# Two transformer layers on one core: reordering the first permutes and norms, gated up products together, first queries on GpSimd, sigmoid by tanh

## Chip, cores and metric

The kernel runs on one core of one Trainium2 chip. The metric is the device time of one execution in microseconds (us); lower is better. An engine is named as the profile names it: PE (TensorE, matmuls), PEld (its weight loads), DVE (VectorE), ACT (ScalarE), POOL (GpSimd), SP (SyncE, which only issues DMAs here).

## The reference, cut to what matters

Two layers act on x of 2 batches x 1024 tokens x 256 features, all in float32. Each layer adds an attention and a feed-forward branch of the same normalized x:

```python
xn = _layernorm(x)
x = x + _L0_attn_ref(xn, ...) + _L0_ffn_ref(xn, ...)
xn = _layernorm(x)
x = x + _L1_attn_ref(xn, ...) + _L1_ffn_ref(xn, ...)
```

Layer 0's attention has 16 heads of width 16 with a causal mask. The reference reshapes the projected (tokens, features) matrix straight into (heads, tokens, 16), so that a head is a block of 64 tokens with all features; the kernel has to permute. Layer 0's feed-forward uses ternary weights (the sign times the mean magnitude of a group of 64), a squared relu and an rms norm. Layer 1's attention is latent: queries from 192 and keys and values from 64 latent columns, 16 heads, rotary positions on 64 columns of each head. Layer 1's feed-forward quantizes its three weights to -1, 0 and 1 and computes

```python
hidden = jax.nn.sigmoid(x @ w1q.T) * (x @ w2q.T)
return hidden @ w3q.T
```

## The kernel before

Tokens lie in 16 tiles of 128 rows (0 to 7 are batch 0, 8 to 15 are batch 1), kept in `x_sb`. The program is one hand-written order: each call issues its instructions at that place into the in-order queues of the engines, and Tile adds the semaphores. An engine that waits therefore holds back everything that was issued to it later. PSUM is handed out as three single banks (`ps_bank`, tile `ps_m`), two pairs (`ps_pair`, `ps_s`) and one accumulator (`ps_o`).

**The start.** Statistics of x (`ln_stat`: two DVE instructions a tile), their square root on ACT (`ln_root`), the reciprocal on DVE (`ln_rstd`), the normalized tile (`ln_norm`, two tiles at once, into the single buffer `xn`; on POOL for most of the head), and its transposes on PE with the copy to `xnT` on ACT (`ln_turn`). `project(g, i)` computes keys (i=1), queries (0) or values (2) of head group g and writes them to DRAM (`rows`); `fetch` reads them back in head order into `stage`; `permute` copies them to `head` tiles. Group g reads only even tiles of its batch for the first two groups and only odd ones for the next two. `first_w` and `second_w` are the four steps (`begin`, `scale`, `choose`, `put`) that make a piece of layer 0's feed-forward weights ternary.

**The first maxima.** Layer 0's softmax takes two passes: `maxima` (PE scores, then DVE reductions to `nmx`), later `scores` with the exponential on ACT, and `product` with the values. A loop over groups g runs from -1 and in it over n = 0 to 11; it computes the maxima of group g+1 beside the scores of group g. At g = -1 there are only maxima, and the dictionary `first` lists for each n what is issued with them: turns and norms of the remaining tiles, projections, `fetch` and `permute`, and eight ups of layer 0's feed-forward. An up is PE products, three ACT passes (relu, square, square) and an accumulation on POOL (`acc`, L541). The four steps of two more weight pieces are dealt over n as well, after the entry of `first`.

**The fill.** From g = 0 on, a list `fill` supplies one piece of independent PE work a step: projections, layer 0's feed-forward, and from g = 5 layer 1's feed-forward of batch 0 (`ffn1(0)`, `ffn1(1)`, 512 tokens each). `ffn1(n)` has 12 ups (six columns, each as product with w1, sigmoid on ACT, product with w2, multiplication on DVE) and 8 downs (six products each, added to `x_sb` on DVE).

**Between the layers.** After the last product of layer 0 a loop over eight tiles of batch 1 does `project_out`, takes pieces of `fill`, and takes pieces of `side`: `down1` (the latent products of layer 1, one tile each). Then batch 1 is normalized and turned, `ffn1(2)` and `ffn1(3)` become the fill, and `side` holds the rest of layer 1's preparation: `norms1` and `keys1` (mostly POOL), `queries1` (transposes), `fold` (products of weights, each with DMA loads two folds ahead), `turn_keys`. When few pieces of fill are left, the buffer of w1 is given to the encoding weights `wpe` and the tables of cosines, and the first two queries are issued: `project` (32 matmuls), copies on ACT, and `rotate` (two multiplications and four additions of pieces, on the engines that it is given).

**Layer 1's attention** loops over 16 steps of pairs of token blocks: scores, maxima on DVE, exponential on ACT, 32x32 transposes on DVE, products. It starts with the two first queries.

Of the kernel before, what the change touches and what calls it, by code (L numbers as in the profile page):

```python
# [17 lines left out]
F32 = mybir.dt.float32  # L18
BF16 = mybir.dt.bfloat16
AF = mybir.ActivationFunctionType  # L20
ALU = mybir.AluOpType
# [25 lines left out]
def two_layers(ctx: ExitStack, tc: tile.TileContext, a: dict, out: bass.AP):  # L47
# [142 lines left out]
    with ExitStack() as scope:  # L190
# [135 lines left out]
        def project(g, i, engine=nc.scalar):  # L326
# [16 lines left out]
            nc.sync.dma_start(  # L343
# [316 lines left out]
        def ffn1(n):  # L660

            f = {}

            def up(hc, i):
                if i == 0 and hc % 2 == 0:
                    f[hc // 2] = l0t.tile([P, 2, SC], F32, tag="four", name="hid", bufs=4)
# [7 lines left out]
                if i == 0:  # L674
                    f["sg"] = l0t.tile([P, SC], F32, tag="acc", name="sg")
                    nc.scalar.activation(f["sg"], pw, AF.Sigmoid)
                else:
                    nc.vector.tensor_tensor(f[hc // 2][:, hc % 2, :], f["sg"], pw, ALU.mult)

            def down(t, e):  # L680
# [8 lines left out]
                nc.vector.tensor_tensor(xt, xt, po[:, :P], ALU.add)  # L689
# [138 lines left out]
        with tc.manual_schedule():  # L828
# [26 lines left out]
            second_w[3]()  # L855
            ln_turn(xnT, 1, turns.pop(), 2)
            turns.append(ln_norm(5, 2, nc.gpsimd))
# [4 lines left out]
            ln_stats(even1)  # L862
            ln_rstd(even1)

            def odd_ones():
                ln_stats(odd1)
                ln_rstd(odd1)


            up = lambda: fill_up.pop(0)()  # L870
# [516 lines left out]
```

## Time and profile before

| what | value |
|---|---|
| median of 3 runs | 1332.9 us (1329.65 to 1333.25) |
| the profiled execution | 1324.88 us |
| its span, first to last instruction | 1323.2 us |
| granted PE clock, mean of the span | 0.990 |
| PE busy | 1267.6 us, 96% of the span |
| DVE / ACT / POOL busy | 750.9 / 675.3 / 478.0 us |
| first maxima start, first scores of group 0 start | 30.4 us, 80.2 us |
| last product of layer 0 ends, first scores of layer 1 start | 574 us, 713.2 us |

A busy PE is not a PE at its peak: matmuls are pipelined, their ends are modelled, and a slower granted clock shows as longer matmuls, not as idle time. So idle time, the releaser named beside it, and the duration of equal groups of matmuls have to be read together. A float32 matmul appears as two records. In lines of the timeline, the first two numbers are start and duration in us, and the bracket is the engine's idle time before the line and what ended it.

### The profile page before, as it was taken

The numbers are of one execution on the slowest core, as the hardware profiler recorded it, in microseconds if no ns is written. First come the engines' busy times: TensorE is split into PE (matmuls) and PEld (weight loads), VectorE is DVE, ScalarE is ACT, GpSimd is POOL, SyncE is SP. The second block draws the span as 40 slices with busy tenths as digits, with TensorE's granted clock in tenths as the row PEclk, the third lists the DMA queues.
The fourth block names the chain that finished last, engine by engine and source line by source line (L and its number), as shares of the span: only waits on it lengthen the run. The fifth ranks groups of instructions, "written<-read, shape, count | busy, mean of one in ns | idle before, by whom it ended". The sixth has DMA issues, their size and how long they took to land.

```text
span 1323.2 us, 36659 instructions
## 1 busy us (share of the span) xinstructions
PE 1267.6 (96%) x15790; PEld 794.5 (60%) x15790; DVE 750.9 (57%) x1879; ACT 675.3 (51%) x1252; POOL 478.0 (36%) x506
## 2 busy tenths in 40 slices
PE   7999999999999999998997899999999999999997
PEld 6554645545546445365765557777666677777665
DVE  5666455656455564134335667656657667666672
ACT  3465447375455664743324555555555555555541
POOL 6553315344232221002132444443444344444320
PEclk9899999999999999999999999999999999999999
DMA  7221301011001000002132200000000000000000
GB/s 234 57 56 57 96 1 25 6 21 17 8 1 25 25 0 25 13 0 60 35 114 55 35 18 11 26 11 6 27 10 27 7 26 11 27 11 6 23 7 22
DMA packets 65809, 41.12 MB, mean 31 GB/s; under 512 B 37840, under 2 KB 63184, under 8 KB 65392
## 3 DMA queue, kind: packets, MB, share of 16 engines
q1 hardware_dynamic: 64800, 35.51, 10.6%
q8 instruction: 124, 2.03, 0.6%
q0 software_dynamic: 416, 2.49, 0.5%
q10 hardware_dynamic: 432, 0.79, 0.2%
q14 instruction: 37, 0.30, 0.1%
HBM read 26.18 MB, written 10.49 MB: 28 GB/s over the span
## 4 chain that ended last, share of the span: by engine, by line
PE 84%; DVE 7%; ACT 4%; issue 3%; POOL 1%; DMA 0%; SPq 0%; ACTq 0%; DVEq 0%; POOLq 0%
PE ps_s L1150 15%; PE ps_m L404 12%; PE ps_o L1198 11%; PE ps_o L470 5%; PE ps_m L669 5%; PE ps_m L558 5%; PE ps_t L146 4%; PE ps_m L527 4%; PE ps_t L1225 4%; PE ps_m L684 3%; PE ps_m L331 3%; PE ps_t L139 3%; DVE p L1157 2%; DVE pT L1167 1%; PE ps_m L707 1%
## 5 line engine op out<-in xcount | busy, mean ns | idle before, releaser
L1161 ACT ACTIVATE p<-p,nmax 128x1024 f32<-128x1024 f32 (+7 forms) x256 | 197.2, 771 | 206.5 <-DVE nmax L1157 205.7
L1150 PE MATMUL ps_s<-kT,qc 128*128 128x512 f32 (+3 forms) x768 | 280.2, 500 | 13.0 <-DVE nmax L1157 11.7
L1157 DVE CUSTOM_DVE_ANT_0 p<-ps_s,wpe 128x1024 f32<-128x1024 f32 (+7 forms) x256 | 185.0, 745 | 181.6 <-PE ps_s L1150 176.8
L452 ACT ACTIVATE p<-ps_s 128x1024 f32<-128x1024 f32 (+1 forms) x192 | 152.8, 809 | 140.6 <-PE ps_s L445 135.5
L1150 PEld LDWEIGHTS ps_s<-kT,qc 128*128 128x128 f32 x768 | 131.8, 191 | 123.1 <-issue 91.8
L1167 DVE STREAM_TRANSPOSE pT<-p 128x1024 f32<-128x1024 f32 (+7 forms) x256 | 186.5, 758 | 13.2 <-ACT p L1161 13.2
L404 PE MATMUL ps_m<-head,head 16*128 16x512 f32 (+3 forms) x672 | 178.3, 532 | 3.4 <-DVE nmx L415 1.3
L445 PE MATMUL ps_s<-head,head 17*128 17x512 f32 (+3 forms) x768 | 167.7, 533 | 1.1 <-ACT p L452 1.1
L1198 PE MATMUL ps_o<-pT,vrep 32*64 32x128 f32 x9216 | 151.3, 275 | 6.5 <-issue 2.8
L1198 PEld LDWEIGHTS ps_o<-pT,vrep 32*64 32x64 f32 x9216 | 134.7, 131 | 34.2 <-issue 25.8
L174 POOL TENSOR_TENSOR qc<-t,t 32x512 f32<-32x512 f32 x120 | 152.1, 1268 | 8.1
L455 POOL TENSOR_SCALAR_AFFINE_SELECT p<-p 128x256 f32<-128x256 f32 x128 | 53.2, 420 | 236.1 <-ACT p L452 235.4
L169 POOL TENSOR_TENSOR t<-t,cosq 128x512 f32<-128x512 f32 x28 | 35.6, 1273 | 258.8 <-issue 144.1
L404 PEld LDWEIGHTS ps_m<-head,head 16*128 16x128 f32 x672 | 67.2, 183 | 88.1 <-issue 29.2
L669 PE MATMUL ps_m<-xnT,w 128*128 128x512 f32 x192 | 93.7, 616 | 0.0
L420 DVE TENSOR_REDUCE nmx<-ps_m 128x1 f32<-128x512 f32 x112 | 72.3, 686 | 33.3 <-PE ps_s L445 25.4
L415 DVE CUSTOM_DVE_ANT_0 junk<-ps_m,maskz,nmx 128x512 f32<-128x512 f32 (+3 forms) x112 | 57.7, 549 | 48.2 <-PE ps_s L445 30.4
L470 PE MATMUL ps_o<-p,v 128*32 128x512 f32 (+3 forms) x768 | 82.4, 501 | 0.3 <-POOL p L455 0.3
L558 PEld LDWEIGHTS ps_m<-wpr,hT 128*128 128x128 f32 x512 | 59.9, 191 | 17.9 <-DVE nmx L420 6.8
L415 DVE CUSTOM_DVE_ANT_0 junk<-ps_m,maskz 128x512 f32<-128x512 f32 (+3 forms) x112 | 50.6, 488 | 30.3 <-PE ps_s L445 27.2
L1225 PE MATMUL ps_t<-wvo,xT 128*128 128x256 f32 x256 | 63.1, 389 | 3.9 <-DVE nmax L1157 2.6
L558 PE MATMUL ps_m<-wpr,hT 128*128 128x128 f32 x512 | 66.6, 282 | 0.0
(184 smaller groups left out, 1779.3 us busy)
## 6 DMA issues: line engine op xcount, KB each, us to landing
rows<-proj SPq DMA_DIRECT2D x24, 256.0 KB, 2.5
stage<-rows SPq DMA_DIRECT2D x96, 64.0 KB, 3.1
w<-in_w SPq DMA_DIRECT2D x3, 768.0 KB, 5.1
x_sb<-in_x SPq DMA_DIRECT2D x4, 512.0 KB, 11.9
x<-x_sb SPq DMA_DIRECT2D x4, 512.0 KB, 3.2
fold_wo<-in_wo SPq DMA_DIRECT2D x8, 256.0 KB, 3.3
vrep<-kv SPq DMA_DIRECT2D x32, 64.0 KB, 2.2
xin<-x SPq DMA_DIRECT2D x16, 128.0 KB, 2.2
```

The lines of the kernel that those rows point to most:

```text
L174: (even, odd)[x].tensor_tensor(self.qc[64 + 32 * x : 96 + 32 * x, hh], t1[at : at + 32], t2[at : at + 32], ALU.add,)
L404: nc.tensor.matmul(t[:, :w], quad(q, c, D0)[:, i * P : (i + 1) * P], quad(k, c, D0)[:, k0 : k0 + w], start=True, stop=True, tile_position= ...
L445: nc.tensor.matmul(t[:, c % 2, :w], quad(k, c, D0 + 1)[:, j * P : (j + 1) * P], quad(q, c, D0 + 1)[:, at : at + w], start=True, stop=True, ...
L452: nc.scalar.activation(p[:, pair[0] : pair[0] + 2, :w], t[:, :, :w], AF.Exp)
L470: nc.tensor.matmul(quad(box["o"], c)[:, SC - w :], values[g][:, j, 32 * c : 32 * c + 32], p[:, c, :w], start=(j == 0), stop=(j == 4 * iq + ...
L558: nc.tensor.matmul(po[:, :P], f["h", hc // 2][:, hc % 2, t * P : (t + 1) * P], wpr[:, hc, cols], start=(hc == 0), stop=(hc == NH0 - 1),)
L669: nc.tensor.matmul(pw, w1t[f"w{i + 1}"][:, kc, hc * P : (hc + 1) * P], xnT1[n // 2][:, kc, (n % 2) * SC : (n % 2 + 1) * SC], start=(kc == ...
L1150: nc.tensor.matmul(sc[:, j * SC + n0 : j * SC + n1], s.q[k].qc[:, h // QP, h % QP, :], kT[:, s.b * S + n0 : s.b * S + n1], start=True, sto ...
L1157: nc.vector.tensor_tensor_reduce(p, sc[:, j * SC : j * SC + w], maskw[:, S - w :], -1.0, 3.0e38, ALU.add, ALU.min, nmax,)
L1161: nc.scalar.activation(p, p, AF.Exp, bias=nmax, scale=-1.0, accum_out=s.rsum[:, k, h : h + 1])
L1167: nc.vector.transpose(s.pT[:, at, h, :], s.p[k, h])
L1198: nc.tensor.matmul(s.o[64 * hh : 64 * hh + 64, c, k * P : (k + 1) * P], vrep[32 * c : 32 * c + 32, s.b * 32 + sb, :], s.pT[32 * c : 32 * c ...
```

## The change

1. The rows of `project(0, 0)`, the first queries, are written to DRAM from ACT's queue instead of SP's.
2. In the start, `project(1, 0)`, both first permutes and `project(1, 2)` are issued ahead of the turn of tiles 1 and 3 and of the next norm; `second_w[3]` is issued after these. The block of batch 1's even statistics ahead of the maxima is gone.
3. In the first maxima, batch 1's statistics are issued one tile at a time (`ln_stat`), with a square root and a reciprocal for each pair of tiles (`root`); norms, turns, projections and ups get other places.
4. Layer 1's gate takes tanh(z/2) instead of the sigmoid: sigmoid(z) = (tanh(z/2) + 1)/2. DVE forms (tanh + 1) times the second product, and the down product is halved where it is added to `x_sb`.
5. Batch 1's statistics between the layers are issued one tile per `project_out`, and the loop's pieces of `fill` and `side` are dealt otherwise (six of fill and seven of side in place of eight and four).
6. All 24 ups of `ffn1(2)` and `ffn1(3)` come ahead of all 16 downs. The hidden tiles of `ffn1(3)` beyond the first two columns go into a buffer of tag `p`.
7. `side` is spread evenly over the fill, and the encoding weights, the tables and the first queries are issued with 16 pieces of fill left instead of 8. Both queries' `rotate` runs wholly on POOL; before, the first ran on DVE and the second on POOL and DVE.

```diff
-            nc.sync.dma_start(
+            queue = nc.scalar if (g, i) == (0, 0) else nc.sync
+            queue.dma_start(
                 rows[g, i].rearrange("(m p) t -> p m t", p=P), proj.rearrange("p (m t) -> p m t", m=2)
             )
...
                 if i == 0 and hc % 2 == 0:
-                    f[hc // 2] = l0t.tile([P, 2, SC], F32, tag="four", name="hid", bufs=4)
+                    if n < 3 or hc == 0:
+                        f[hc // 2] = l0t.tile([P, 2, SC], F32, tag="four", name="hid", bufs=4)
+                    else:
+                        if hc == 2:
+                            f["two"] = l0t.tile([P, 4, SC], F32, tag="p", name="hid", bufs=3)
+                        f[hc // 2] = f["two"][:, hc - 2 : hc]
...
-                    nc.scalar.activation(f["sg"], pw, AF.Sigmoid)
+                    nc.scalar.activation(f["sg"], pw, AF.Tanh, scale=0.5)
                 else:
-                    nc.vector.tensor_tensor(f[hc // 2][:, hc % 2, :], f["sg"], pw, ALU.mult)
+                    nc.vector.scalar_tensor_tensor(
+                        f[hc // 2][:, hc % 2, :], f["sg"], 1.0, pw, ALU.add, ALU.mult
+                    )
...
-                nc.vector.tensor_tensor(xt, xt, po[:, :P], ALU.add)
+                nc.vector.scalar_tensor_tensor(xt, po[:, :P], 0.5, xt, ALU.mult, ALU.add)
...
             second_w[2]()
-            second_w[3]()
-            ln_turn(xnT, 1, turns.pop(), 2)
-            turns.append(ln_norm(5, 2, nc.gpsimd))
             permute(0, 1)
             project(1, 0)
             permute(0, 0)
             project(1, 2, nc.vector)
-            ln_stats(even1)
-            ln_rstd(even1)
-            def odd_ones():
-                ln_stats(odd1)
-                ln_rstd(odd1)
+            ln_turn(xnT, 1, turns.pop(), 2)
+            turns.append(ln_norm(5, 2, nc.gpsimd))
+            second_w[3]()
+            def root(n):
+                at = slice(n, n + 3, 2)
+                ln_root(at)
+                ln_rstd(at)
...
             first = {
-                0: [lambda: ln_turn(xnT, 5, turns.pop(), 2), odd_ones,
-                    lambda: turns.append(ln_norm(8, 2, nc.gpsimd))],
-                1: [lambda: fetch(0, 2), lambda: project(2, 1), up],
-                2: [lambda: ln_turn(xnT, 8, turns.pop(), 2), lambda: project(2, 0), up,
-                    lambda: turns.append(ln_norm(12, 2, nc.gpsimd))],
-                3: [lambda: project(2, 2), up],
-                4: [lambda: permute(0, 2), lambda: fetch(1, 1), lambda: fetch(1, 0),
-                    lambda: ln_turn(xnT, 12, turns.pop(), 2), up],
-                5: [lambda: project(3, 1), lambda: turns.append(ln_norm(9, 2, nc.gpsimd))],
-                6: [lambda: project(3, 0)],
-                7: [lambda: permute(1, 1), lambda: ln_turn(xnT, 9, turns.pop(), 2), up,
-                    lambda: turns.append(ln_norm(13, 2, nc.gpsimd))],
-                8: [lambda: permute(1, 0), up],
-                9: [lambda: project(3, 2), lambda: ln_turn(xnT, 13, turns.pop(), 2)],
-                10: [up],
-                11: [up],
+                0: [lambda: turn_norm(5), lambda: project(2, 1)],
+                1: [lambda: fetch(0, 2), up],
+                2: [up, lambda: ln_stat(8)],
+                3: [up, lambda: ln_stat(10), lambda: root(8)],
+                4: [lambda: permute(0, 2), lambda: fetch(1, 1), lambda: fetch(1, 0), up,
+                    lambda: norm(8), lambda: ln_stat(12)],
+                5: [lambda: project(2, 0), lambda: turn_norm(8), lambda: project(2, 2),
+                    lambda: ln_stat(14), lambda: root(12)],
+                6: [lambda: project(3, 1), lambda: norm(12), lambda: ln_stat(9)],
+                7: [lambda: permute(1, 1), lambda: turn_norm(12), lambda: project(3, 0),
+                    lambda: ln_stat(11), lambda: root(9)],
+                8: [lambda: permute(1, 0), up, lambda: norm(9), lambda: ln_stat(13)],
+                9: [up, lambda: turn_norm(9), lambda: project(3, 2), lambda: ln_stat(15),
+                    lambda: root(13)],
+                10: [up, lambda: norm(13)],
+                11: [up, lambda: turn_norm(13)],
             }
...
-                if i % 2 == 0 and fill:
+                if i < 6:
                     pump()
-                    pump()
-                elif side:
+                for _ in range((0, 1, 0, 1, 0, 1, 2, 2)[i]):
                     side.pop(0)()
+                if i > 0:
+                    ln_stat(TB + i - 1)
                 if i == 4:
-                    ln_stats(four(2))
+                    ln_root(four(2))
...
             rest()
-            ln_stats(four(3))
+            ln_stat(NT - 1)
+            ln_root(four(3))
             ln_rstd(four(3))
...
-            fill += ffn1(2) + ffn1(3)
+            two, three = ffn1(2), ffn1(3)
+            up2 = 2 * HC1
+            fill += two[:up2] + three[:up2] + two[up2:] + three[up2:]
...
                 k = len(fill)
                 pump()
-                if first > 0:
-                    first -= 1
-                    n = 1 if len(side) > 26 else 0
-                else:
-                    n = -(-len(side) // k)
-                for _ in range(n):
-                    if side:
-                        side.pop(0)()
-                if k == 9:
+                for _ in range(-(-len(side) // k)):
+                    side.pop(0)()
+                if k == 17:
                     wpe = main.tile([P, 8 * E], F32, tag="wC", name="wpe")
...
                         q.project(ps_pair())
-                        v, p = nc.vector, nc.gpsimd
                         q.rotate(
-                            (p, v, p) if k else (v, v, v),
-                            [temp("t").rearrange("p (r t) -> p r t", r=QP) for _ in range(2)],
+                            room=[temp("t").rearrange("p (r t) -> p r t", r=QP) for _ in range(2)]
                         )
```

More of the change, by code (lines that the diff above doesn't have):

```diff
@@ L861, in two_layers @@
             project(1, 2, nc.vector)
-            ln_stats(even1)
-            ln_rstd(even1)
-            def odd_ones():
-                ln_stats(odd1)
-                ln_rstd(odd1)
-            up = lambda: fill_up.pop(0)()
+            ln_turn(xnT, 1, turns.pop(), 2)
[5 more added lines that the diff above has]
+                ln_rstd(at)
             fill_up = fill[12:20]
@@ L872, in two_layers, with up @@
             del fill[12:20]
[L873 to L889 removed]
+            def up():
+                fill_up.pop(0)()
@@ new lines, in norm, with turn_norm @@
+            def norm(n):
+                turns.append(ln_norm(n, 2, nc.gpsimd))
+            def turn_norm(n):
+                ln_turn(xnT, n, turns.pop(), 2)
+            first = {
+                0: [lambda: turn_norm(5), lambda: project(2, 1)],
[14 more added lines that the diff above has]
+                11: [up, lambda: turn_norm(13)],
@@ L1052, in two_layers @@
             side += [lambda n=n: turn_keys(1, n) for n in (0, 4)]
-            first = len(fill) - 40
             while fill:
@@ L1056, in two_layers @@
                 pump()
-                if first > 0:
-                    first -= 1
-                    n = 1 if len(side) > 26 else 0
-                else:
-                    n = -(-len(side) // k)
-                for _ in range(n):
-                    if side:
-                        side.pop(0)()
-                if k == 9:
+                for _ in range(-(-len(side) // k)):
+                    side.pop(0)()
+                if k == 17:
                     wpe = main.tile([P, 8 * E], F32, tag="wC", name="wpe")
```

## Prediction

> **What bounds the kernel now.** I read the page's shares first, then busy time by stage, then the timeline of each stage that the edits touch. The page says TensorE:
>
> ```profile
> PE 1267.6 (96%) x15790; PEld 794.5 (60%) x15790; DVE 750.9 (57%) x1879; ACT 675.3 (51%) x1252; POOL 478.0 (36%) x506
> ```
>
> The missing 4% is not spread evenly. Cut at my own stage borders, the windows view (length, PE busy, PEld, DVE, ACT, POOL, granted clock, DMA share, GB/s) gives:
>
> ```profile
> 20.00:30.40 10.40, 4.91 (x27) 3.51 (x25) 6.79 (x13) 3.72 (x4) 9.17 (x7) 1.00 0.70 182
> 30.40:80.20 49.80, 48.07 (x214) 25.68 (x214) 33.81 (x100) 24.08 (x40) 27.06 (x21) 0.90 0.23 53
> ...
> 440.00:574.80 134.80, 130.79 (x815) 55.34 (x815) 51.50 (x147) 84.64 (x101) 25.66 (x48) 0.99 0.05 15
> 574.80:609.60 34.80, 31.04 (x188) 25.66 (x189) 16.38 (x56) 8.99 (x34) 0.00 (x0) 0.95 0.20 57
> 609.60:693.10 83.50, 82.60 (x406) 52.16 (x404) 30.62 (x86) 26.87 (x80) 24.21 (x34) 1.00 0.19 59
> 693.10:713.20 20.10, 14.75 (x133) 13.70 (x133) 9.23 (x16) 7.04 (x11) 5.87 (x4) 0.96 0.00 1
> ```
>
> Five stages have holes, and the edits touch all five. Idle also hides as slow clock: one `project` takes 1.99 us at 55.4 and 3.50 at 60.2.
>
> Head: timeline around the first maxima (start, duration, work, idle before it and its releaser):
>
> ```profile
> 16.57 0.60 ACT L339 ACTIVATE proj<-ps_m 128x512 f32<-128x512 f32 x1 [1.67 <-PE ps_m L331]
> 19.31 1.81 SPq L353 DMA_DIRECT2D stage<-rows  x4
> 21.22 0.40 SPq L343 DMA_DIRECT2D rows<-proj  x1
> 24.03 1.78 SPq L353 DMA_DIRECT2D stage<-rows  x4
> 28.37 1.94 ACT L362 COPY head<-stage 128x1024 f32<-128x1024 f32 x1 [1.96 <-DMA stage<-rows]
> 30.37 1.14 PE L404 MATMUL ps_s<-head,head 16*128 16x512 f32 x8 [2.87 <-ACT head L362]
> ```
>
> The queries' rows are ready at 17.17, but SP, standing in the keys' fetch, sends them at 21.22.
>
> Tables, the batch-1 turn, and the queries' turn:
>
> ```profile
> 537.51 1.28 ACT L676 ACT_TABLE_LOAD   x1
> 539.41 1.28 ACT L452 ACT_TABLE_LOAD   x1
> 541.79 2.04 PE L445 MATMUL ps_s<-head,head 17*128 17x512 f32 x8 [0.85 <-ACT p L452]
> ...
> 606.01 1.09 PE L281 MATMUL ps_m<-ident,xn 128*128 128x128 f32 x4 [2.39 <-DVE xn L270]
> ...
> 708.02 2.35 DVE L174 TENSOR_TENSOR qc<-t 32x512 f32<-32x512 f32 x2 [3.44 <-POOL t L170]
> 710.74 2.02 PE L684 MATMUL ps_m<-w,hid 128*128 128x128 f32 x12 [3.58 <-DVE x_sb L689]
> ```
>
> The last pair is one story: VectorE waits 3.44 us for GpSimd with the down products' adds queued behind it, so no PSUM bank comes free and TensorE stands.
>
> **What the Trainium skill says.** "ScalarE: Activation LUTs", section "Table sets: the hidden batching unit", puts exp and tanh in one set, sigmoid's anchor in another. Its section "What ACT_TABLE_LOAD costs" gives 1283 ns and a drain of 1380 ns per switch; the trace has the 1283, but the activation starts 0.02 us after the load (441.09+1.28, then 442.39), so I price 1.3. "DMA: Bandwidth & Descriptors", "Issuing engines are not separate DMA queues", says that another issuing engine saves only the sequencer's time; here that time is 4.05 us (17.17 to 21.22). "GPSIMD Engine Reference", "Elementwise — side-by-side cycle accounting", has GpSimd at 2.6 cycles an element on two inputs; the trace has 1.27 us (POOL L169) against 0.69 (DVE). "TensorE: Matmul & The Clock Gate", "What's actually happening", says that an idle window of about 3.4 us halves the clock; the trace shows clocks of 0.66 to 0.68 after the holes at 57 and 603.
>
> **Head, part by part.** (a) The rows go out on ScalarE's queue at 17.2 (one issue, 0.4 us, ahead of 1.2 us of weight work there). They land at about 20, inside SP's own keys' fetch, so the queries' fetch starts at 21.2 instead of 24.0: 2.8 us. The permute stands ahead of the turn now, so the first maxima start at 27.6. `project(1,0)` and `(1,2)` move ahead of the turn's wait (1.85+0.77) into the hole. `second_w[3]` is late by some 6 us on POOL (27.1 to 29.9) but needed only by the first up, about 33.
>
> (b) Batch 1's statistics: eight of 0.58 us leave two blocks. The first stood at 28.2 to 30.4 under ScalarE's copy, at no cost; the second (34.1 to 36.3) delayed reductions. Dealt out, all eight compete with the maxima's reductions (2.47 us a step), and each `root` puts a reciprocal into VectorE's queue behind a square root, which stands in ScalarE's queue behind its slot's other work. In slot 3 that is relu, square, square (1.97 us): VectorE is shut for about 2 us and the reductions queue behind.
>
> (c) A norm (two halves, 2.42 us on POOL) is now turned one slot after it is issued, not two, and three of the four stand behind an up's accumulation. From the start of an up to the end of such a norm it is 1.9 (products) + 2.1 (three activations) + 1.27 + 2.42 = 7.7 us, which the trace shows (44.28 to 51.98). TensorE has less to do meanwhile. Laying slots 0 to 11 out by hand from 27.6, at full clock, TensorE waits 3.6 us at `turn(8)`, 2.5 at `turn(9)`, 3.2 at `turn(13)`, and about 4 for reductions. The first scores come at 83.8, against 80.2 now: **3.6 us later**. I add 1.4 for one slow clock, half of what the slow spell at 57.8 to 63.3 costs today (about 3). Head: **-5**. Bounds: +3 if the norms are ready in time, so that (a) survives; -12 if every wait draws a slow spell.
>
> **Tanh.** 30 loads, 15 at L676 and 15 of 18 at L452, are 39 us of ScalarE. Most lies under TensorE. On the path I find 1.1 us of scores waiting for L452, 0.3 for L676 and the slow clock at 543.8 to 548 (products 3.06 for 1.98 us, then about 0.5): 3.0 at most, **+2.5** taken, 0.5 below. The VectorE forms change: L678 is 0.69, the nearest rows are 0.69 to 0.87; 24 times 0.1 hides under 1.7 us products.
>
> **Batch 1's turn (574.8 to 609.6).** TensorE's work at its pitches: transposes 0.6 and 8 x 0.22, 8 projections x 0.9, 8 downs x 1.34, 6 latent downs x 1.07, 4 turns x 0.45 = 28.3 of 34.8 us. Now the statistics run one per token, so behind the last projection stand add, one statistic, root, reciprocal, norm = 2.6 us, and TensorE has a latent down and a down, 2.4, to cover it. The second norm (0.8) lies under the other down. Two more latent downs move in (2.1). New length about 31.4 for work that takes 36.9 now: **+5.5** (3 to 6.5).
>
> **Main loop.** `norms1` starts earlier; today's 0.9 at 627 becomes about 0.4: +0.5. After it, all ups come before all downs; the second hidden tiles go into the third `p` buffer, idle here since the scores ended, so no new wait. The last weight loads on SP now stand behind the encoding weights and four tables (2.3 us of issue, and these wait for the last up), and land about 7.5 us after that up where the last fold wants them at 7.4: -0.5, at worst -1.5.
>
> **First queries.** The query block is hung at 16 remaining downs instead of 8, so query 0 now has eight downs behind it, not five. From its start TensorE has two queries (2 x 2.87), two transposes (0.86) and eight downs (10.7) = 17.3 us, where today it has five downs and 13.3 us of work, and takes 20.1. On GpSimd query 0 is ready at 6.2 (product, copies) + 2 x 1.27 + 5.25 = 14.0, query 1 at 21.8; its scores could start at 21.7, because the first reduction waits for the store of x either way (3.3 us today). VectorE no longer waits, so no add is late. Saving 20.1-13.3 = 6.8, **+6** after a margin. If GpSimd takes 1.7 us an add, as the two at 708 did beside VectorE, 3.3 is lost again: 3 to 7.
>
> **Sum.** -5 + 2.5 + 5.5 + 0.5 - 0.5 + 6 = **+9 us**. The profiled execution took 1324.9 (span 1323.2), so its like becomes 1315.9. The median of the runs stands 8.0 higher; I take the same 9 off it: 1332.9 - 9 = **1323.9**.
>
> **Rivals.** *The head is free*: norms end before their turns, (a) stays. For it: POOL is only half busy in the head. Against: 7.7 us per chain. 9+5+3 = 17 saved, 1316. *The head eats nearly everything, or tanh buys nothing* (placed in a set without exp, loads stay): saving 0 to 4, about 1331. *The head costs more than all the rest brings*, the slower end: four turns and the roots each start a half-clock spell of 3 us and the spells feed the next wait. The rest brings 14, so first scores at 80.2+14+4 = 98 decide; 83.8 and four spells give 96, so a little more is needed: about 1338. Against it: the same stage has two spells today and still a mean clock of 0.90.
>
> **How the numbers follow.** My case has 0.60, the free head 0.17, the near nothing 0.15, the slower 0.08. About 0.3% (4 us) is what a measurement can tell from no change; my case's tail lends 0.03 to "same" and the near-nothing gives 0.03 to "faster". Range: head +3 with the upper ends elsewhere is about 20 saved, 1313; head -12 with the lower ends is about 2 lost, 1335.
>
> **What would show it.** First maxima at 27 to 28; waits L281 <- POOL xn of 2 to 4 us three times in the head; first L445 at 82 to 86. L676 without loads; scores at 541 without a wait. The 2.39 us at L281 gone; the waits of L684 on L689 gone and L174 wholly on POOL. If first L445 comes before 78, my head is wrong; if the queries' stage still waits, the cover is.

## The result, and the profile after

The changed kernel takes 1316.34 us (median of 16 runs, 1313.13 to 1323.16), the kernel before, run beside it, 1324.89 (median of 16, 1319.26 to 1333.25): a ratio of 0.9938, with a 95% interval from 0.9912 to 0.9964. That is 8.6 us off, where 9 were predicted. The 1332.9 shown earlier was the median of three runs and lay at the upper end of the sixteen, so the predicted time itself stands 7.6 us above the measured one. The profiled execution took 1319.51 us (span 1317.4).

The page of the changed kernel still says TensorE, with 34 us less work for ScalarE:

```profile
PE 1268.4 (96%) x15790; PEld 797.0 (60%) x15790; DVE 744.2 (56%) x1873; ACT 641.3 (49%) x1227; POOL 487.2 (37%) x514
```

I cut both spans at the same five events: first maxima, first scores, first tile of the loop between the layers, first up of the main loop, first reduction of layer 1.

| stretch | before, us | after, us | after less before |
|---|---|---|---|
| start to first maxima | 30.37 | 28.80 | -1.57 |
| to first scores of group 0 | 49.82 | 57.99 | +8.17 |
| to the first tile between the layers | 495.08 | 490.74 | -4.34 |
| to the first up of the main loop | 34.37 | 33.21 | -1.16 |
| to the first reduction of layer 1 | 106.75 | 98.08 | -8.67 |
| to the end | 606.81 | 608.58 | +1.77 |

Up to the first reduction that is 7.6 us; the last stretch has the same code in both. The windows view of the changed kernel at its own borders (length, PE busy, PEld, DVE, ACT, POOL, granted clock, DMA share, GB/s) shows where TensorE stands now:

```profile
20.00:28.80 8.80, 4.53 (x23) 3.75 (x22) 3.63 (x5) 3.19 (x4) 7.72 (x6) 1.00 0.88 179
28.80:86.80 58.00, 50.98 (x213) 25.86 (x214) 36.02 (x109) 26.32 (x45) 29.50 (x24) 0.88 0.21 46
...
440.00:577.00 137.00, 136.34 (x888) 59.35 (x886) 58.14 (x163) 58.50 (x82) 26.16 (x49) 0.99 0.05 15
577.00:610.70 33.70, 31.93 (x196) 26.33 (x197) 17.97 (x63) 11.13 (x48) 0.04 (x1) 1.00 0.01 1
610.70:686.90 76.20, 76.20 (x362) 46.69 (x360) 28.40 (x75) 21.91 (x64) 24.05 (x34) 1.00 0.27 84
686.90:705.20 18.30, 17.84 (x169) 17.28 (x169) 4.12 (x11) 5.75 (x10) 11.62 (x10) 1.00 0.09 30
```

The four later stages have lost most of their holes: idle is 0.7 us at the end of layer 0 (4.0 before) and 0.5 in the queries' stage (5.4). The head has gained them: 7.0 us idle in the second line, against 1.7, and a lower clock.

Timeline of the changed kernel's start (start, duration, work, idle before it and its releaser):

```profile
17.42 0.39 ACTq L345 DMA_DIRECT2D rows<-proj  x1
...
19.68 3.77 SPq L355 DMA_DIRECT2D stage<-rows  x8
...
26.80 1.95 ACT L364 COPY head<-stage 128x1024 f32<-128x1024 f32 x1 [3.80 <-DMA stage<-rows]
```

The rows leave 3.8 us earlier and SP issues the eight fetches in one piece, as predicted. But the permute starts 1.6 us earlier, not 2.8. From the last issue to the permute 3.35 us pass, where it was 2.56 (25.81 to 28.37). The fetches now run in one stretch (DMA share 0.88 where it was 0.70), which may be why; no run tests it.

Later in the same head:

```profile
48.75 0.38 PE L302 MATMUL ps_m<-q_ab,half 128*128 128x512 bf16 x1 [1.64 <-ACT q_ab L296]
...
74.60 0.44 PE L281 MATMUL ps_m<-ident,xn 128*128 128x128 f32 x2 [1.12 <-POOL xn L270]
75.80 0.44 PE L281 MATMUL ps_m<-ident,xn 128*128 128x128 f32 x2 [0.76 <-POOL xn L270]
85.21 0.44 PE L281 MATMUL ps_m<-ident,xn 128*128 128x128 f32 x2 [1.90 <-POOL xn L270]
86.41 0.44 PE L281 MATMUL ps_m<-ident,xn 128*128 128x128 f32 x2 [0.77 <-POOL xn L270]
```

The last four lines are the turns of tiles 9 (1.9 us in two pieces) and 13 (2.7 us) waiting for their norms on POOL, at the places and nearly of the sizes that were predicted (2.5 and 3.2). The first line is a wait for a weight piece that was not laid out. On POOL, ahead of tile 9's turn:

```profile
72.07 1.27 POOL L543 TENSOR_TENSOR acc<-acc,sq 128x512 f32<-128x512 f32 x1 [3.69 <-ACT sq L542]
73.32 2.43 POOL L270 TENSOR_SCALAR xn<-x_sb,ln_mv,ln_rstd 128x256 f32<-128x256 f32 x2
```

POOL stands still for 3.7 us, because the up's accumulation waits for its square and the norm is issued behind it.

The queries' end of the changed kernel:

```profile
697.87 6.86 PE L696 MATMUL ps_m<-w,hid 128*128 128x128 f32 x60
...
703.58 5.21 POOL L174 TENSOR_TENSOR qc<-t 32x512 f32<-32x512 f32 x4
705.21 3.67 PE L1164 MATMUL ps_s<-kT,qc 128*128 128x512 f32 x8 [0.47 <-DVE x_sb L701]
708.82 1.23 DVE L1171 CUSTOM_DVE_ANT_0 p<-ps_s,wpe 128x1024 f32<-128x1024 f32 x1 [3.76 <-POOL qc L174]
709.25 0.38 SPq L703 DMA_DIRECT2D x<-x_sb  x1
```

The downs run without a gap, and the additions are wholly on POOL. The fourth line is a wait that was not predicted: the first reduction starts 0.03 us after POOL's last addition, and ahead of the store of x, for which, by the prediction, it would wait.

### The profile page after: what moved, and what is told of

Same layout as the page of the kernel before. It is cut to its first block, busy times and chain, and to the rows that moved or that the text cites. A ratio compares the mean times of both kernels' runs of the same rounds, so it can differ in the third digit from the quotient of the medians.

```text
span 1317.4 us, 36641 instructions
## 1 busy us (share of the span) xinstructions
PE 1268.4 (96%) x15790; PEld 797.0 (60%) x15790; DVE 744.2 (56%) x1873; ACT 641.3 (49%) x1227; POOL 487.2 (37%) x514
## 5 line engine op out<-in xcount | busy, mean ns | idle before, releaser
L417 DVE CUSTOM_DVE_ANT_0 junk<-ps_m,maskz,nmx 128x512 f32<-128x512 f32 (+3 forms) x112 | 57.6, 548 | 46.9 <-PE ps_s L447 29.5
```

The lines of the kernel that those rows point to most:

```text
L417: nc.vector.tensor_tensor_reduce(junk[:, :w], t[:, :w], maskz[:, SC - w :], -1.0, dst if k0 else 3.0e38, ALU.add, ALU.min, dst,)
```

## The experiments

Each kernel differs from the changed one by the edit shown, unless the text says otherwise. Single executions of the same code scatter, so I read stages in one trace of each kernel. The ratio beside them is that of the medians to the kernel before, run at the same time, with its 95% interval; the changed kernel has 0.9938.

**1. The whole old head** (parts 1 to 3 undone; the dictionary `first` is that of before as well).

```diff
-            queue = nc.scalar if (g, i) == (0, 0) else nc.sync
+            queue = nc.sync
...
+            second_w[3]()
+            ln_turn(xnT, 1, turns.pop(), 2)
+            turns.append(ln_norm(5, 2, nc.gpsimd))
             permute(0, 1)
             project(1, 0)
             permute(0, 0)
             project(1, 2, nc.vector)
-            ln_turn(xnT, 1, turns.pop(), 2)
-            turns.append(ln_norm(5, 2, nc.gpsimd))
-            second_w[3]()
+            ln_stats(even1)
+            ln_rstd(even1)
...
```

> The changed kernel with the whole start of the kernel before (parts 1 to 3 undone: rows on SP's queue, permutes behind the turn, statistics in blocks, the old order of the first maxima); parts 4 to 7 stay. In the changed kernel the first scores of group 0 started at 86.8, before at 80.2. Theory (the new head costs what the trace shows): first scores back at 80 to 81, and some 7 to 9 us off the end, since a third half-clock spell (86.8 to 95) also goes: about 1308 to 1310 where the changed kernel took 1316.3. Rival 1 (the late head is made good later, because the stage behind it waits for the weights or the fetches anyway): less than 2 us off. Rival 2 (the clock spells move elsewhere): first scores at 80, but the stage from there to the last product of layer 0 is 3 us longer than the changed kernel's 490.3, so only 4 off.

Measured: first scores at 80.30, the stage behind them 487.3 (490.7 in the changed kernel); median 1309.08, ratio 0.9875 (0.9852 to 0.9899). Rivals 1 and 2 fall: the head's loss is real, is not made good later, and reaches 3 us into the next stage. In that stage the granted clock is halved for 13.7 us in the changed kernel, 6.8 of them from 87.3 on, and for 3.4 us here.

**2. New start, old order of the maxima** (part 3 alone undone: the diff of experiment 1 from `ln_stats(even1)` on, with the dictionary of before).

> The changed kernel with its own start (parts 1 and 2: rows on ACT's queue, permutes ahead of the turn), but with the order of the first maxima and the statistics in blocks of the kernel before (part 3 undone). Theory (the permutes' gain is real and the new order of the maxima loses it): first maxima at 28.8 as in the changed kernel, first scores 1.6 earlier than with the old start, at 78.5 to 79; total about 1307 to 1309. Rival (the early start is lost in any order, because the first block of statistics and the turn of tiles 1 and 3 now stand between the first reductions): first scores at 80 to 82, no better than with the old start.

Measured: first maxima 28.45, first scores 79.27; ratio 0.9867 (0.9841 to 0.9893), median 1309.25. The start seems to keep about 1.0 of its gain at the first scores (79.27 against 80.30), between theory and rival; two traces whose stages scatter by as much cannot settle it. So all of the head's loss sits in the new order of the maxima: 57.99 us for it, 50.82 for the old order with the new start.

**3. Norms and roots ahead of the ups.**

```diff
-                3: [up, lambda: ln_stat(10), lambda: root(8)],
+                3: [lambda: ln_stat(10), lambda: root(8), up],
-                4: [lambda: permute(0, 2), lambda: fetch(1, 1), lambda: fetch(1, 0), up,
-                    lambda: norm(8), lambda: ln_stat(12)],
+                4: [lambda: norm(8), lambda: permute(0, 2), lambda: fetch(1, 1),
+                    lambda: fetch(1, 0), up, lambda: ln_stat(12)],
-                8: [lambda: permute(1, 0), up, lambda: norm(9), lambda: ln_stat(13)],
+                8: [lambda: norm(9), lambda: permute(1, 0), up, lambda: ln_stat(13)],
-                9: [up, lambda: turn_norm(9), lambda: project(3, 2), lambda: ln_stat(15),
-                    lambda: root(13)],
+                9: [lambda: ln_stat(15), lambda: root(13), up, lambda: turn_norm(9),
+                    lambda: project(3, 2)],
-                10: [up, lambda: norm(13)],
+                10: [lambda: norm(13), up],
```

> The changed kernel, only the order inside the slots of the first maxima changed: in slots 4, 8 and 10 the norm is issued ahead of the up (so that POOL does it before the up's accumulation), and in slots 3 and 9 the square root is issued ahead of the up's three ACT passes. Theory (turns wait because their norm stands behind an accumulation, and reciprocals because their root stands behind an up): the waits of TensorE at the turns of tiles 9 (1.9 us) and 13 (2.7 us) go, with them the half-clock spells behind them; first scores at 80 to 83 instead of 86.8; total about 1310 to 1313. Rival (the reductions on VectorE are the bound in the head, and the statistics dealt among them cost the time): first scores between 85 and 87, total within 2 us of 1316.

Measured: no wait at the turns of tiles 9 and 13, first scores at 80.56; median 1307.79, ratio 0.9874 (0.9836 to 0.9913). The wait at 48.75 for the weight piece is gone too, but tile 8's turn now waits 1.5 us. The same work with the same number of statistics among the reductions takes 5.7 us less, so the rival (reductions as the bound) falls.

**4. The norms alone**: slots 4, 8 and 10 as in experiment 3, slots 3 and 9 as in the changed kernel.

```diff
-                10: [up, lambda: norm(13)],
+                10: [lambda: norm(13), up],
...
```

> The changed kernel with only the norms of slots 4, 8 and 10 issued ahead of their up; the square roots stay behind the ups of slots 3 and 9. With both edits the first scores came at 80.6 instead of 86.8. Theory as in the prediction (the chain up, accumulation, norm is what the turns wait for): the waits at the turns of tiles 9 and 13 (1.9 and 2.7 us) shrink to under 1 each, first scores at 82 to 83.5; what the roots cost (VectorE shut for 2.1 in slot 3 and TensorE's 1.6 at 48.7) stays. Rival 1 (the late roots are the cause, since a norm also waits for its reciprocal): waits and first scores stay within 1.5 of the changed kernel's. Rival 2 (the norms do all of it): 80 to 81.

Measured: first scores at 81.20, no turn waits in the second half; median 1310.0, ratio 0.9861 (0.9799 to 0.9924). From first maxima to first scores 53.1 us, against 52.3 with both edits and 58.0 with neither: the norms are worth 4.9, the roots 0.8. The first agrees with the 4.6 us of waits that went. The second is no more than a hint: the three traced executions with the old head have 49.0 to 50.1 us there. That the norms were also moved ahead of two permutes on POOL does not explain it: in the changed kernel the permute ahead of tile 9's norm ends at 68.4, and POOL then waits for the up. Timeline of this kernel's VectorE:

```profile
45.60 0.17 DVE L260 RECIPROCAL ln_rstd<-ln_rstd 128x2 f32<-128x2 f32 x1 [2.11 <-ACT ln_rstd L252]
59.03 0.17 DVE L260 RECIPROCAL ln_rstd<-ln_rstd 128x2 f32<-128x2 f32 x1 [4.71 <-ACT ln_rstd L252]
```

The reciprocals still shut VectorE for 2.1 and 4.7 us, and by that pair of traces it costs 0.8 us: these are long waits on an engine that is mostly not on the path.

**5. The sigmoid back** (part 4 undone), and **6. tanh alone on the kernel before** (the same lines the other way round).

```diff
-                    nc.scalar.activation(f["sg"], pw, AF.Tanh, scale=0.5)
+                    nc.scalar.activation(f["sg"], pw, AF.Sigmoid)
...
```

> The changed kernel with the sigmoid in place of tanh (part 4 undone: sigmoid, plain multiplication, plain addition). Theory as in the prediction: 2.5 us longer, so the stage from first scores to the last product of layer 0 goes from 490.3 to 492.8, total about 1319. Rival 1 (all table loads are hidden under TensorE): 0 to 0.5 us longer. Rival 2 (the 30 loads cost more, since that stage also holds a half-clock spell from the head worth about 3 us, which hides part of tanh's gain in the comparison of the two traces): 6 to 7 us longer, total about 1323.

> The kernel before with part 4 alone (tanh, the three VectorE forms). Taken back from the changed kernel, this part made the stage from first scores to the last product of layer 0 6.3 us longer, where the prediction had 2.5. Theory (6.3 is its own worth and does not depend on the other parts): the stage, 495.1 us in the kernel before (80.2 to 575.3), becomes 488 to 490, head and later stages unchanged, total about 1319. Rival (2.5 as predicted; the rest came from where the clock's spells fell in those two executions): 492 to 493, total 1322 to 1323.

Measured: with the sigmoid back, the stage from first scores to the loop is 497.06 (490.74), main loop and queries unchanged (98.07 against 98.08), median 1328.18, ratio 1.0018 (1.0001 to 1.0035). Alone on the kernel before, the stage falls from 495.08 to 487.21; median 1320.7 beside 1328.45, ratio 0.9951 (0.9929 to 0.9972). Rival 2 of the first expectation holds, and the rival of the second falls. The two figures, 6.3 and 7.9 us, agree once the slow clock is counted (its loss put at half the length of its spells): half clock takes 1.7 us of the stage in both traces of experiment 6, but 5.1 us with the sigmoid back and 6.8 us in the changed kernel. So tanh is worth about 8 us at equal clock. The ratios of whole executions give 10.6 us for experiment 5 (uncertain by some 4) and 6.5 for experiment 6 (by some 3). Groups of table loads by line, changed kernel:

```profile
L454 ACT ACT_TABLE_LOAD x6 | 7.7, 1283 | 3.9 <-PE ps_s L447 3.8
...
L686 ACT ACT_TABLE_LOAD x2 | 2.6, 1283 | 0.0
```

and with the sigmoid back:

```profile
L454 ACT ACT_TABLE_LOAD x18 | 23.1, 1283 | 18.6 <-PE ps_s L447 18.4
L686 ACT ACT_TABLE_LOAD x14 | 18.0, 1283 | 1.5 <-PE ps_m L679 1.3
```

That is 24 loads fewer at these two lines; the prediction had all 30 gone. Idle TensorE accounts for 3.3 us (4.0 us from 440 to the end of the stage with the sigmoid, 0.7 without). As much again is hidden in busy TensorE. Timeline with the sigmoid back, and last an equal group of the changed kernel:

```profile
548.55 1.28 ACT L454 ACT_TABLE_LOAD   x1
549.84 1.94 ACT L454 ACTIVATE p<-ps_s 128x1024 f32<-128x1024 f32 x2
550.92 2.04 PE L447 MATMUL ps_s<-head,head 17*128 17x512 f32 x8 [0.85 <-ACT p L454]
...
545.48 1.14 PE L447 MATMUL ps_s<-head,head 17*128 17x512 f32 x8
```

The group of score products takes 0.90 us longer at full clock, because its second half waits for the exponential that the table load has delayed (it ends at 551.78). No idle time shows inside the group, as the ends of matmuls are modelled. Four such groups (2.04, 2.04 and 1.65 us for 1.14, and 1.83 for 0.93) make 3.2 us. The remaining 1.4 us lie in the products just ahead of waits.

**7. Old engines for the first queries' rotation** (query 0 on VectorE, query 1 shared), all else as changed.

```diff
+                        v, p = nc.vector, nc.gpsimd
                         q.rotate(
+                            (p, v, p) if k else (v, v, v),
-                            room=[temp("t").rearrange("p (r t) -> p r t", r=QP) for _ in range(2)]
+                            [temp("t").rearrange("p (r t) -> p r t", r=QP) for _ in range(2)],
```

> The changed kernel, only the engines of the first two queries' rotation as before (query 0 wholly on VectorE, query 1 on GpSimd with half of its additions on VectorE); order of the fill and place of the queries stay changed. In the changed kernel query 0 starts at 686.9 and layer 1's first scores at 705.2, 18.3 us later, and the first reduction then waits 1.9 us for GpSimd. Theory (VectorE must be free for the downs' adds): query 0 shuts VectorE for some 6 to 7 us and query 1 for some 5, the three PSUM banks fill, TensorE waits again; 18.3 becomes 21 to 23 us. Rival (the place with eight downs behind is what counts, GpSimd costs rather than helps): 18.3 stays within 0.5, and the first reduction comes 1.9 us earlier because GpSimd ends earlier.

Measured: 25.4 us from query 0 to layer 1's first scores, even more than expected; ratio 0.998 (0.9955 to 1.0006). Timeline:

```profile
701.77 2.35 DVE L174 TENSOR_TENSOR qc<-t 32x512 f32<-32x512 f32 x2 [3.45 <-POOL t L170]
701.81 3.43 POOL L174 TENSOR_TENSOR qc<-t 32x512 f32<-32x512 f32 x2
...
704.50 7.25 PE L696 MATMUL ps_m<-w,hid 128*128 128x128 f32 x48 [3.59 <-DVE x_sb L701]
```

The stall of the kernel before is back: VectorE waits for POOL, an add behind it is late, TensorE waits for the bank. The first reduction now comes 2.2 us after the first scores (3.6 in the changed kernel), so the rival is right on that one point, with 1.4 us in place of 1.9. The two engines also slow each other: VectorE's addition takes 0.70 alone (2.78 for four, at 694.36) and 1.18 here, POOL's 1.30 alone and 1.72 here. The Trainium skill, "SBUF — State Buffer", section "Who interferes with whom", says that a VectorE instruction with two SBUF inputs contends with a GpSimd one that reads SBUF; these numbers agree.

**8. The whole old end of the fill** (parts 6 and 7 undone), and **9. the old place with the new engines** (as 8, but `rotate` as in the changed kernel).

```diff
-            two, three = ffn1(2), ffn1(3)
-            up2 = 2 * HC1
-            fill += two[:up2] + three[:up2] + two[up2:] + three[up2:]
+            fill += ffn1(2) + ffn1(3)
...
-                if k == 17:
+                if k == 9:
...
```

> The changed kernel with the whole end of layer 1's fill as before (parts 6 and 7 undone: ups and downs of the two blocks in turn, the side pieces bunched, queries at 8 remaining pieces, rotation engines as before). From the first up of the main loop to layer 1's first scores the changed kernel took 94.5 us, the kernel before 103.6, of which 2.1 are two latent products that have moved ahead. Theory: 101 to 102 us, 7 longer than changed, with the waits of the down products on their adds and of VectorE on POOL's products back; total about 1323. Rival (part of the 7 comes from tanh, whose table loads no longer stand beside the ups): 97 to 99 us.

> The changed kernel with order of fill and place of the queries as before (8 pieces left), but both rotations on GpSimd as in the changed kernel. Measured to the first reduction of layer 1 from the first up of the main loop: changed 98.1 us, with old engines and old place 104.2, with old engines and new place 103.7. Theory (GpSimd needs 21.9 us from the start of query 0 to its last addition, in any place, and the first reduction waits for that): query 0 starts 80.9 after the first up as in the old place, the first reduction at 102.8, with a wait of 5 to 6 us on GpSimd; so new engines alone bring 1.4 and the place the rest. Rival 1 (engines are all that counts): 98 to 99. Rival 2 (a place too late makes GpSimd worse than VectorE): over 104.2.

Measured, from the first up to the first reduction: 104.22 in experiment 8 (first scores after 100.80, close to the theory), 102.74 in experiment 9, 98.08 in the changed kernel; ratios 0.9973 (0.9952 to 0.9994) and 0.9989 (0.9962 to 1.0017). Timeline of experiment 9:

```profile
707.26 3.67 PE L1164 MATMUL ps_s<-kT,qc 128*128 128x512 f32 x8 [0.47 <-DVE x_sb L696]
...
714.85 1.23 DVE L1171 CUSTOM_DVE_ANT_0 p<-ps_s,wpe 128x1024 f32<-128x1024 f32 x1 [7.74 <-POOL qc L174]
```

POOL's last addition ends 21.8 us after query 0 started (692.99 to 714.82), as in the changed kernel. With that constant the theory had 102.8. So the engines alone bring 1.5, the place with the new order of the fill 0.5 (experiment 7 has 103.74), all together 6.1: each needs the other. The two small figures are not told apart, since half clock takes 1.7 us of that stretch in experiments 7 and 8 and 0.2 in 9. The place and the order of the fill were not parted.

**10. The old loop between the layers** (part 5 undone).

```diff
-                if i < 6:
+                if i % 2 == 0 and fill:
                     pump()
-                for _ in range((0, 1, 0, 1, 0, 1, 2, 2)[i]):
+                    pump()
+                elif side:
                     side.pop(0)()
-                if i > 0:
-                    ln_stat(TB + i - 1)
...
```

> The changed kernel with the loop between the layers as before (part 5 undone: pieces of fill in pairs on even tiles, batch 1's statistics in two blocks). From the first transposes of that loop to the first up of the main loop the changed kernel took 33.7 us with 8 latent products, the kernel before 34.9 with 6, so 3.3 us of gain where 5.5 was predicted. Theory (3.3 is all there is): 35 us with 6 latent products, the 2.1 us of the other two coming back in the main loop, and a wait of 2 to 2.5 us at the third turn. Rival 1 (the prediction's 5.5 was right, the comparison was disturbed by clock or place): 37 us. Rival 2 (the latent products that moved were hidden work anyway): main loop not longer, net 1.2 us or less.

Measured: 34.0 us in the loop, the 2.4 us wait back, median 1328.36, ratio 1.0009 (0.9978 to 1.0039). Timeline:

```profile
609.88 0.67 PE L281 MATMUL ps_m<-ident,xn 128*128 128x128 f32 x4 [2.40 <-DVE xn L270]
...
718.95 1.23 DVE L1170 CUSTOM_DVE_ANT_0 p<-ps_s,wpe 128x1024 f32<-128x1024 f32 x1 [7.76 <-POOL qc L174]
```

From the first tile to layer 1's first reduction it takes 139.8 us, 8.5 more than the changed kernel, more than any of the three expected. Of these, 0.3 lie in the loop, 2.1 in the two latent products that follow it, about 4 in the reduction's longer wait (7.76 for 3.76). The first scores come 14.3 us after query 0, not 18.3, because three downs fewer stand behind it, and POOL still needs 21.9 us; three side pieces more ahead of the queries are the likely reason. The rest, some 2, is slow clock behind the 2.4 us wait (the next up takes 2.82, not 1.98).

**11. Idle products ahead of the first maxima, queries earlier**, on top of experiment 2.

```diff
             second_w[3]()
+            keep_warm(12)
...
-                    side += last[:2] + [lambda: query(0), last[2], lambda: query(1), last[3]]
+                    side += [lambda: query(0), last[0], lambda: query(1)] + last[1:]
```

> Two additions to the kernel that keeps the changed start but the old order of the first maxima (its first maxima 28.5, first scores 79.3, layer 1's first scores 18.3 us after query 0). (1) Twelve idle products of 0.28 us on TensorE in the hole ahead of the first maxima (24.5 to 28.4), whose results nobody reads. Theory: the hole is what draws the half clock from 29 to 38, which costs 4.7 us by the granted clock (0.50 and 0.55 in two windows of 5 us), so first scores at 74.5 to 76. Rival: the reductions on VectorE hold that stage as well, and only 1 to 2 us come off; or the half clock comes for another reason and nothing does. (2) Both queries are issued ahead of most of the last transposes, some 3.5 us earlier. Theory: GpSimd's last addition ends before the first scores do, and the wait of the first reduction on it (1.9 us) goes. Rival: the wait is for something else, the reduction stays 3.6 us after the first scores. Total by theory about 1302, by the rivals 1306 to 1308.

Measured: median 1301.34 (1296.14 to 1304.78), ratio 0.9792 (0.9749 to 0.9835). The queries' part holds: the first reduction comes 2.2 us after the first scores, released by TensorE, and the stretch from the first up is 96.66 (98.08). The clock's part fails: first scores at 78.96, 0.3 better. So the total that the theory gave (1302) was met by luck. The stages account for 1.7 us, while the median is 7.9 below that of experiment 2; what made the rest is not shown.

**12. More idle products**, on top of experiment 11.

```diff
-            keep_warm(12)
+            keep_warm(15)
...
-                    lambda: turns.append(ln_norm(8, 2, nc.gpsimd))],
+                    lambda: turns.append(ln_norm(8, 2, nc.gpsimd)), lambda: keep_warm(4)],
```

> The last kernel with idle products ahead of the first maxima, with 15 of them instead of 12 and 4 more behind slot 0 of the first maxima, so that TensorE has no gap over 0.3 us from 22 to 40. There the half clock still came, from 31.8 to 38.6, after 3 us later gaps of 0.85 and 0.81 us. Theory A (any gap ahead of it draws the half clock): no spell up to 40, first scores at 75.5 to 76.5 instead of 79.0. Theory B (the hole only moves the spell; something else about this stretch, such as products that use 16 of 128 rows, draws it): the spell stays 6 to 7 us long, first scores between 78.5 and 80.

Measured: first scores at 75.08, with the full clock all the way to them. Windows of experiment 11, then of experiment 12 (columns as above):

```profile
32.00:36.00 4.00, 4.00 (x12) 1.93 (x11) 3.50 (x16) 1.00 (x3) 1.37 (x2) 0.50 0.01 2
36.00:40.00 4.00, 4.00 (x11) 2.40 (x9) 1.45 (x8) 0.93 (x2) 0.00 (x0) 0.71 0.05 16
```

```profile
32.00:36.00 4.00, 3.86 (x15) 2.50 (x16) 3.50 (x16) 1.74 (x4) 0.59 (x1) 1.00 0.00 0
36.00:40.00 4.00, 4.00 (x24) 2.62 (x23) 3.66 (x15) 1.92 (x5) 1.04 (x1) 1.00 0.20 70
```

Theory A holds here: in experiment 11 gaps of 0.85 and 0.81 us were left, and the spell came 2 us later than in experiment 2. It is one trace, but the thirteen others all have gaps there and all show a spell that begins between 27.6 and 33.3 us. The whole run shows nothing of the 3.9 us: the median is 1300.94 over four runs (1300.90 to 1308.14), the ratio 0.9807 (0.9753 to 0.9861), not told apart from experiment 11. Both are faster than the changed kernel.

## Why the prediction came out right

**Head, predicted -5; measured -6.6 at the first scores** (86.79 against 80.19). Mechanism and place were right, as experiments 3 and 4 show. Of the 1.6 us that are missing, 1.2 lie in (a): 1.6 was gained instead of 2.8. The stage from the first maxima was nearly met, 58.0 us where 57.6 was laid out (83.8 less 27.6, and 1.4 for a slow clock), but in part by luck. The layout had 13.3 us of waits at full clock; the trace has 7.0 us idle and 6.8 us lost to half clock. The 3.6 us at tile 8's turn is an example: the products ahead of it run at half clock here and nothing waits, while in experiment 5, whose spell lies later, that turn waits 2.5 us. Six of the executed kernels have the changed head, with first scores from 86.79 to 91.35, mean 88.2; three have the old one, at 80.19 to 80.69. So the head costs 7.8 on the mean, and a spell behind its last wait (from 87.3 in the changed kernel) reaches some 3.4 into the next stage, which was not predicted. Item (b), VectorE shut by the reciprocals, was real and nearly free (0.8).

**Tanh, predicted +2.5; +4.3 in the pair of traces, about 8 by itself.** The prediction added up the waits that name a table load's line (1.4) and a slow spell (1.6), and set 3.0 as a ceiling. The spell was no part of it: it stands elsewhere in the stage in experiment 6, where half clock takes 1.7 us as before. The waits were too few: the windows shown had 4.0 us of idle TensorE there, and the group at 541.79, 2.04 us long, already held a wait that no view calls idle. The pair of traces shows 4.3 because half clock takes 6.8 us of that stage after the change and 1.7 before.

**Batch 1's turn, the main loop and the first queries, predicted +5.5, 0 and +6; measured 9.8 together** (1.16 + 8.67). Counting the work that changed places (two latent products, 2.1 us, and three downs, 4.0 us), the turn brought 3.3, the main loop 1.1 and the queries 5.4. The steps were right: the 2.39 us wait gone, two latent products moved in, no down held up by an add for more than 0.2 us. The loop itself takes 33.7 us where 31.4 was laid out; four waits of 0.28 to 0.64 us for the latent products' squares on ScalarE make up 1.6 of it. The queries' stage takes 18.3 us where 17.3 stood, and GpSimd needs 21.9 us for both queries, as the prediction had it (21.8). The wrong step is "the first reduction waits for the store of x either way". In experiment 11 it starts as soon as its scores are there, and in the changed kernel ahead of the store. So 1.4 us were left on GpSimd.

**Sum.** +9 predicted, 7.6 in the stages, 8.6 in the medians. The closeness is partly luck: errors of opposite sign, tanh taken too small, the head's clock and the turn taken too kindly, nearly cancel. The free head (first scores before 78) did not happen. Of the near nothing, one half (tanh buys nothing) is contradicted by the 24 loads gone and by experiments 5 and 6; the other half is near the truth, since the head eats most of what tanh brings. Without its loss the change would have been about twice as good (experiments 1 to 4).

What stays open: why a spell of slow clock begins where no gap, or hardly one, stands ahead of it (below), and why experiment 11 gained more in its median than in its stages.

## What to carry to other kernels

A producer on an in-order queue has to be issued ahead of the long work that it must not wait for: moving three norms ahead of three ups was worth 5 us. For the gain of an edit, neither the waits that carry its name (1.4 us for tanh) nor the idle time of its stage (4.0) is a ceiling, when the edit brought 8: compare the duration of equal groups of matmuls as well, for a wait inside a group shows only there. And a slow engine can take work off a busy one only where enough work lies behind it: engine and place apart brought at most 1.5 us, together 6.1.

## What the runs showed of the hardware

A spell of half clock needs no gap. In eight of the fourteen traces, all of them with tanh, one product of an up between 482 and 497 us runs at half clock for 3.4 us, with TensorE busy all through the 7 us before. Windows of the changed kernel there (columns as above):

```profile
490.00:493.50 3.50, 3.50 (x31) 1.79 (x29) 1.51 (x4) 1.62 (x2) 2.42 (x2) 1.00 0.00 0
493.50:497.00 3.50, 3.50 (x8) 1.18 (x4) 1.29 (x2) 1.50 (x2) 2.21 (x2) 0.51 0.00 0
```

Ahead of it stand products that use 16 or 17 of 128 rows or 32 of 128 columns; whether these draw the spell is not tested. The longest spell, in experiment 12, began at 306 us, behind a single gap of 0.34 us, and lasted to 323 with TensorE busy throughout. A window within it:

```profile
312.00:316.00 4.00, 4.00 (x26) 3.12 (x28) 0.74 (x4) 0.00 (x1) 1.10 (x2) 0.50 0.00 0
```

Half of it is lost, some 8.5 us, and the stage took 496.2 us where experiment 11, with the same instructions and the same gap of 0.34 us, took 487.0. So such a gap does not always draw a spell either. The Trainium skill, "TensorE: Matmul & The Clock Gate", section "What's actually happening", puts the half clock down to an idle window of about 3.4 us. The hole of 4.3 us ahead of the first maxima in the changed kernel agrees with that. The two spells above do not, nor do those ahead of or in the first maxima of experiments 3 and 11, behind holes of 2.5 and 0.85 us, nor those that the prediction read behind waits of 0.37 and 2.39 us.

Inside the traces, the record of the granted clock knows full and half speed alone, and its spells of half clock last 3.41, 6.83, 10.24, 13.65 or 17.07 us, multiples of 3.41 us. They also bound what one profile can tell. From the first reduction of layer 1 to the end, the same code took between 602.6 and 612.1 us in the fourteen executions profiled, as much as the whole change is worth. Half clock takes between 0 and 10.1 us of that stretch; without it, 601.0 to 603.9 us are left. So most of the scatter between executions is slow clock.
